# A graph layer on one core: the first gathers' pacing, the node loads' place, and the last tiles' self connection

## The chip, the cores and the metric

The kernel runs on one core of a Trainium2 chip. The metric is device time in microseconds (us), here the median of several executions. Beside it stands one execution taken by the hardware profiler; its span is the time from its first to its last instruction. All arithmetic is float32.

## What is computed

One message-passing layer over a graph of 12500 nodes and 400000 edges, the edges sorted by destination. Each node has 160 features: 64 scalars s and 32 vectors v of three components. Cut to what matters:

```python
h_s, h_v = s @ lin1_ws * a, v @ lin1_wv * a            # per node: the table that is gathered
w = silu(edge_attr_64 @ fc_w1) @ fc_w2                  # per edge: 224 weights
es, ev = h_s[src], h_v[src]                             # per edge: the source's row
mid = products of w, (es, ev) and the edge's 4 attributes
agg = segment_sum(mid, dst)                             # per node
pre = self connection (s @ sc_ws, v @ sc_wv) * a + (agg @ lin2) * a
out = layernorm(x + [silu(pre scalars), sigmoid(pre gates) * pre vectors])
```

The scale factors are left out here. `node_vec1` is the factor a.

## The kernel before

**Setup.** The table h is computed by TensorE and written to memory (L350 to L369). The destinations are made relative to the first one of each block of three tiles (L419, L424). A tile is 128 edges.

**The loop over quads** (L957) takes four tiles a turn: 782 quads, numbered from 0, the last one with a single tile. For each:

- GpSimd gathers the 4 x 128 rows of h with four indirect DMAs (`gather`, L467, the DMA at L471) into one of five buffers `hg`.
- TensorE computes the hidden layer for two quads at a time (`hidden`, L462; ScalarE's SiLU at L464), four quads ahead, and the quad's weights (`weights`, L546) into one of two PSUM banks `pw`.
- VectorE multiplies weights by gathered rows (`products`, L556 and L564), builds a one-hot matrix of the relative destinations (L609) and multiplies it by the edge's attributes (`select_quad`, L618). The attributes arrive in the order of tiles in `eat` (one buffer, 48 tiles) and are copied by ScalarE into the order of quads in `eas` (`by_slot`, L592 and L600). The copy is made when the first quad of such a group of twelve asks for it, in L618.
- Two quads later TensorE sums the products over the edges with the selection as weights (`add_tile`, L625). A finished pair of blocks is copied by ScalarE (L836), turned (L641, L644), put through the second linear map for up to 16 blocks (L654, L657), and added by VectorE into the accumulator `acc` at the block's first node (L662).

**Nodes.** When all edges of 512 nodes are added up, a job finishes them (`finish`, L665). It issues three loads on SP's queue (xs and xv, the transposed features, L682 and L683; xt, the features themselves, L688). Then come two turns, each for two tiles of 128 nodes: TensorE adds the self connection and the accumulator in PSUM (L700 with xs or xv and the weights scs or scv; L701 with acc and the identity), ScalarE takes the tanh (L703), VectorE gates (L708, L711) and adds the features (L717). Then moments (L725, L727), root (L731), norm (L737) and the store (L740). There are 24 jobs, the last of two tiles, and then the last four tiles by themselves behind all edges: these take three of the gather buffers for xt, xs and xv, because the gathers are done.

**Order.** It is written out by hand: each engine runs its instructions in program order. `begin` (L940), called once in each quad behind the products, starts the next job if no turn and no later step of the job before is left and the job's nodes are complete. Its loads are issued at once, and its first turn is run in the next quad by `spread_out` (L912), which puts at most one of four kinds of TensorE work (hidden layer, second map, turning of blocks, turn of nodes) into a half quad. In the last seven quads a turn is run as soon as it is there.

**Pacing.** The third gather of a quad carries an extra dependence: it waits until the last weights of the quad two earlier are done. The dictionary `weighed_by` names that instruction, and it is asked with `.get(n - 2)`, so the first two quads have none.

The indices of the gathers (L160), `eat` (L161) and the edge scalars `es` (L205) are loaded eight quads ahead on SP's queue, the queue of the node loads and stores. An alternative that fetches rows by ScalarE's queue is built for every 900th quad and so for none here.

Of the kernel before, what the change touches and what calls it, by code (L numbers as in the profile page):

```python
# [10 lines left out]
F32 = mybir.dt.float32  # L11
# [50 lines left out]
def gnn_kernel(  # L62
# [104 lines left out]
    def index(t):  # L167
        a0, idx, _ = ahead(t)
        return idx[:, t - a0:t - a0 + 1]
# [492 lines left out]
        nc.vector.tensor_add(window, window, os[:, :, b])  # L662


    def finish(fin, psum, t0, nt, p, most=NF, pool=None):  # L665


        whole = nt if p == P else nt - 1
        if pool is None:
            xt = fin.tile([P, most, D], F32, name="xt")  # L670
            xs = fin.tile([S, most * P], F32, name="xs2")
            xv = fin.tile([V3, most * P], F32, name="xv2")
        else:
            xt, xs, xv = (pool.tile([P, Q, D], F32, name="hg") for _ in range(3))
            xs, xv = (a.rearrange("p t d -> p (t d)")[:k, :most * P] for a, k in ((xs, S), (xv, V3)))
        cn = (nt - 1) * P + p
        held = []
        if whole < nt:
            nc.vector.memset(xt[:, whole], 0.0)
            for a in (xs, xv):  # L680
                nc.vector.memset(a[:, whole * P:nt * P], 0.0)
        nc.sync.dma_start(xs[:, :cn], xs_t[:, t0 * P:t0 * P + cn])  # L682
        nc.sync.dma_start(xv[:, :cn], xv_t[:, t0 * P:t0 * P + cn])  # L683
        parts = [(slice(t0 * P, (t0 + whole) * P), slice(0, whole), P)] if whole else []
        if whole < nt:
            parts.append((slice((t0 + whole) * P, (t0 + whole) * P + p), slice(whole, nt), p))
        for nodes_of, k, n in parts:
            nc.sync.dma_start(xt[:n, k], x[nodes_of, :].rearrange("(t p) d -> p t d", p=n))  # L688

        def turn(ks):  # L690
            if not held:
                held.extend(fin.tile([P, most, *shape], F32, name=name) for name, shape in (
                    ("g", [V3]), ("y", [D]), ("st", [6]), ("mv", [2]), ("rs", [])))
            g, y = held[:2]
            pp = psum.tile([P, 2, 2, V3], F32, name="pp", tag="misc")
            for k in ks:
                c = (t0 + k) * P
                for m, (w, a) in enumerate(((scs, xs), (scv, xv))):
                    at_p = pp[:, k % 2, m]
                    nc.tensor.matmul(at_p, a[:, k * P:(k + 1) * P], w, start=True, stop=False)  # L700
                    nc.tensor.matmul(at_p, acc[:, m, c:c + P], ident[:V3, :V3], start=False, stop=True)  # L701
            for k in ks:
                nc.scalar.activation(g[:, k], pp[:, k % 2, 0], AF.Tanh, scale=half_at[:, t0 + k:t0 + k + 1])  # L703
# [24 lines left out]

        def root():
            mv, rs = held[3:]  # L730
            nc.scalar.activation(rs[:, :nt], mv[:, :nt, 1], AF.Sqrt, bias=eps)  # L731

        def norm():
            _, y, _, mv, rs = held
            nc.vector.reciprocal(rs[:, :nt], rs[:, :nt])
            for k in range(nt):
                nc.vector.tensor_scalar(y[:, k], y[:, k], mv[:, k, 0:1], rs[:, k:k + 1],  # L737
                                        op0=OP.subtract, op1=OP.mult)
            for nodes_of, k, n in parts:
# [9 lines left out]
    jobs = [(t, min(NF, tiles_of_nodes - LAST - t), P)  # L749
            for t in range(0, tiles_of_nodes - LAST, NF)]  # L750
    last_job = (tiles_of_nodes - LAST, LAST, N - (tiles_of_nodes - 1) * P)

    with tc.tile_pool(
        name="fin", bufs=1
# [157 lines left out]
        def spread_out(n, half):  # L912
# [5 lines left out]
            while True:  # L918
                kinds = [(q[0][0] + more, k) for k, (q, more) in enumerate(
                    ((hids_due, 2), (maps_due, 3), (turns_due, 1))) if q and q[0][0] <= n]  # L920
                if not late and turning and half == 0:
                    kinds.append((n + 1, 3))
                if not kinds:
                    return rest
# [12 lines left out]
                else:  # L937
                    return turning.pop(0)()

        def begin():  # L940

            if to_do and not turning and not doing:
                t, nt, p = to_do[0]
                end = (t + nt - 1) * P + p
                if not waiting or min(waiting) * RATE >= end + MARGIN:
                    job = finish(fin, misc_ps, *to_do.pop(0))
                    turning.extend(job[:-3])
                    doing.extend(job[-3:])

        with in_order:  # L950
            fetch(0)
# [5 lines left out]
            for n, (c, i, tiles) in enumerate(steps):  # L957
# [9 lines left out]
                fetch(n + LEAD)  # L967
                fetch_rows(n)
                hg = hq_of.pop(n) if n in own else gather(
                    deep, [index(t) for t, _, _ in tiles], {2: weighed_by.get(n - 2)})  # L970
                pw = weights(pw_ps, hids[c, i // 2], [(half, u - i // 2 * 4) for _, half, u in tiles])
                weighed_by[n] = weighed[-1]

                if n + 4 < len(steps) and not steps[n + 4][1] % 2:
                    hids_due.append((n, n + 4))
                rest = spread_out(n, 0)
                step_on = not rest and doing.pop(0) if doing and not turning and not rest else None
                ready = []
# [18 lines left out]
                    add(*a)  # L997
                if step_on:
                    step_on()
                begin()  # L1000
# [29 lines left out]
            while adds:  # L1030
                for a in add_up(n) + add_up(n):
                    add(*a)
            while turning or doing or to_do:
                begin()
                for f in turning:
                    f()()
                for f in doing:
# [120 lines left out]
```

## Time and profile before

| what | us |
|---|---|
| median of 3 executions | 4024.61 |
| lowest, highest | 4024.17, 4026.55 |
| the profiled execution | 4024.39 |
| its span | 4022.6 |
| GpSimd busy | 2990.6 (74%) |
| TensorE busy | 3566.6 (89%) |
| VectorE busy | 2349.4 (58%) |
| ScalarE busy | 847.9 (21%) |

The profile names engines PE (TensorE), PEld (its weight loads, beside PE), DVE (VectorE), ACT (ScalarE), POOL (GpSimd) and SP or SPq (SyncE's DMA queue). A line of its groups reads: line, engine, operation, out<-in, shapes, count | busy us, mean ns of one | idle us just before them and what ended it. A line in order of time reads: start, duration, engine, line, operation, and in brackets the idle time before it and what ended it. A float32 matmul counts twice, since it runs as two passes. The mean granted TensorE clock was 0.931 of full.

### The profile page before, as it was taken

To read this page: it belongs to the slowest core of one execution; us is meant where nothing else is said; L and a number is where in the kernel's file an instruction comes from. 1 tells how busy PE (TensorE), PEld (TensorE's weight loads), DVE (VectorE), ACT (ScalarE), POOL (GpSimd) and SP (SyncE) were. 2 spreads that over 40 slices of the span, in tenths; PEclk is the share of its full clock that TensorE was granted. 3 is DMA by queue.
4 is the path that set the end of the run, shared out by engine and by line. 5 is a ranking of instruction groups with operands and counts; after the bars stand their busy time and mean duration, and the time that the engine had idled before them with its cause. 6 is when DMAs were issued, how large, how long until landed. Compare 5 with 4: busy or idle time off the path is not lost.

```text
span 4022.6 us, 57806 instructions
## 1 busy us (share of the span) xinstructions
PE 3566.6 (89%) x19989; PEld 1993.0 (50%) x19989; DVE 2349.4 (58%) x6410; ACT 847.9 (21%) x1828; POOL 2990.6 (74%) x3172
## 2 busy tenths in 40 slices
PE   6898898988998988898898898998898888888887
PEld 4454454554554544454454454454454444444445
DVE  5555555555655656556565565665655565656654
ACT  2211212212212212122122121221221221212212
POOL 6777777777777777777777777777777777777773
PEclk8898999989999999899898898998999999999998
DMA  7333434434334434344334334434434344343331
GB/s 236 92 95 98 110 91 102 103 98 109 97 98 103 102 98 103 99 101 104 99 94 110 99 98 103 102 97 104 102 95 107 95 103 105 95 107 101 95 100 53
DMA packets 237525, 412.51 MB, mean 103 GB/s; under 512 B 78040, under 2 KB 160961, under 8 KB 237093
## 3 DMA queue, kind: packets, MB, share of 16 engines
q0 software_dynamic: 152960, 266.64, 25.2%
q1 hardware_dynamic: 83668, 141.96, 14.9%
q8 instruction: 159, 2.61, 0.3%
q14 instruction: 144, 1.18, 0.1%
q10 hardware_dynamic: 594, 0.13, 0.0%
HBM read 392.49 MB, written 16.00 MB: 102 GB/s over the span
## 4 chain that ended last, share of the span: by engine, by line
PE 35%; issue 22%; DMA 17%; POOL 16%; DVE 9%; DVEq 0%; SPq 0%; ACT 0%; POOLq 0%; ACTq 0%
DMA hg<-h_tab,idx 16%; POOL hg L471 16%; PE pa L625 11%; PE pw L546 8%; PE misc L641 6%; DVE pr L564 5%; PE misc L654 4%; PE misc L462 3%; PE misc L701 2%; DVE sel L618 1%; PE misc L700 1%; DVE pr L556 1%; DMA xz<-in_xv_t_dram 1%; DVE acc L662 1%; DVE pw L609 0%
## 5 line engine op out<-in xcount | busy, mean ns | idle before, releaser
L471 POOL DMA_INDIRECT hg<-h_tab,idx x3125 | 2960.0, 947 | 963.8 <-issue 812.1
L625 PE MATMUL pa<-pr,sel 128*64 128x416 f32 x6250 | 1330.0, 548 | 0.5 <-DVE sel L618 0.5
L556 DVE TENSOR_TENSOR pr<-pw,hg 128x512 f32<-128x512 f32 x782 | 540.5, 691 | 1198.8 <-DMA hg<-h_tab,idx 885.0
L564 DVE TENSOR_TENSOR pr<-pw,hg 128x384 f32<-128x384 f32 x2346 | 1154.2, 548 | 0.0
L546 PE MATMUL pw<-w,hid 64*128 64x224 f32 x6250 | 837.6, 388 | 258.2 <-DVE sel L618 254.3
L546 PEld LDWEIGHTS pw<-w,hid 64*128 64x128 f32 x6250 | 553.2, 193 | 809.8 <-DVE sel L618 433.3
L625 PEld LDWEIGHTS pa<-pr,sel 128*64 128x64 f32 x6250 | 393.2, 141 | 685.5 <-issue 661.5
L641 PEld LDWEIGHTS misc<-ident,sa 128*128 128x128 f32 x4168 | 526.5, 205 | 76.8 <-issue 73.4
L641 PE MATMUL misc<-ident,sa 128*128 128x96 f32 (+1 forms) x4168 | 553.3, 289 | 0.7 <-ACT sa L836 0.7
L462 PE MATMUL misc<-es,w 128*128 128x512 f32 (+1 forms) x784 | 442.6, 647 | 19.8 <-DVE rel L424 19.3
L464 ACT ACTIVATE hid<-misc 128x512 f32<-128x512 f32 x392 | 233.7, 596 | 922.8 <-PE misc L462 922.6
L644 ACT COPY tt<-misc 128x512 f32<-128x512 f32 (+1 forms) x263 | 153.1, 582 | 1105.8 <-PE misc L641 1105.8
L654 PE MATMUL misc<-tt,l 128*96 128x256 f32 (+5 forms) x1496 | 358.4, 388 | 0.7 <-ACT tt L644 0.5
L609 DVE TENSOR_TENSOR pw<-rel,iota 128x64 f32<-128x64 int16 x782 | 178.8, 229 | 305.5 <-PE pw L546 275.7
L836 ACT COPY sa<-pa 128x416 f32<-128x416 f32 x521 | 263.0, 505 | 328.1 <-PE pa L625 328.1
L618 DVE TENSOR_TENSOR sel<-pw,eas 128x256 f32<-128x256 f32 x782 | 324.5, 415 | 11.7 <-ACT eas L600 9.7
L654 PEld LDWEIGHTS misc<-tt,l 128*96 128x96 f32 (+1 forms) x1496 | 226.8, 165 | 124.6 <-issue 59.4
L701 PE MATMUL misc<-ident,acc 96*128 96x96 f32 x392 | 109.2, 371 | 142.0 <-DVE acc L662 136.1
L662 DVE TENSOR_TENSOR acc<-acc,os 96x32 f32 x1042 | 196.0, 188 | 22.9 <-ACT os L657 4.5
L462 PEld LDWEIGHTS misc<-es,w 128*128 128x128 f32 x784 | 118.0, 190 | 133.8 <-issue 100.1
L701 PEld LDWEIGHTS misc<-ident,acc 96*128 96x128 f32 x392 | 80.9, 256 | 155.0 <-DVE acc L662 139.8
L657 ACT COPY os<-misc 96x512 f32<-96x512 f32 (+2 forms) x68 | 38.4, 564 | 467.8 <-PE misc L654 363.2
(90 smaller groups left out, 671.0 us busy)
## 6 DMA issues: line engine op xcount, KB each, us to landing
es<-in_es_t_dram SPq DMA_DIRECT2D x258, 384.0 KB
hg<-h_tab,idx POOLq DMA_INDIRECT x3125
h_tab<-ht POOLq DMA_DIRECT2D x24, 320.0 KB
xt<-in_x_dram SPq DMA_DIRECT2D x23, 320.0 KB
out_dram<-y SPq DMA_DIRECT2D x23, 320.0 KB
xv<-in_xv_t_dram SPq DMA_DIRECT2D x23, 192.0 KB
eat<-in_ea_dram SPq DMA_DIRECT2D x41, 96.0 KB
xw<-in_xs_t_dram SPq DMA_DIRECT2D x6, 512.0 KB
```

The source lines that it names most:

```text
L462: nc.tensor.matmul(ph[:k, c], w1[:k, :k], es[:k, t0 * P + c0 * P:t0 * P + c1 * P], start=True, stop=True)
L471: got = nc.gpsimd.indirect_dma_start(out=hg[:, t, :], out_offset=None, in_=h_tab, in_offset=bass.IndirectOffsetOnAxis(ap=i, axis=0))
L546: weighed.append(nc.tensor.matmul(pw[:, t, :NWT], hid[r, c * P:(c + 1) * P], w2[r], start=True, stop=True).ins.name)
L556: nc.vector.tensor_mul(two, pw[:, :n, :2 * S].rearrange("p t (k c) -> p t k c", k=2), hg[:, :n, None, :S].to_broadcast([P, n, 2, S]))
L564: nc.vector.tensor_mul(pr[:, :n, first:first + V3].rearrange("p t (i c) -> p t i c", i=3), pw[:, :n, None, 2 * S + k * V:2 * S + (k + 1) * ...
L618: nc.vector.tensor_mul(sel[:, :n], oh[:, :, None, :].to_broadcast([P, n, 4, W]), by_slot(tiles[0][0])[:, u:u + n, :, None].to_broadcast([P ...
L625: summed.append(nc.tensor.matmul(pa[half * ROWS:(half + 1) * ROWS, :NPR], sel[:, t].rearrange("p k w -> p (k w)"), pr, start=start, stop=s ...
L641: nc.tensor.matmul(pt[:, planes, m * n:(m + 1) * n], sa[:k, c:c + P], wanted[:, of, :n], start=True, stop=True)
L654: nc.tensor.matmul(po[:, k, :nb], l2[r, terms[to, part, four]], a[:, :nb], start=(n == 0), stop=(n == len(of) - 1))
L662: nc.vector.tensor_add(window, window, os[:, :, b])
L701: nc.tensor.matmul(at_p, acc[:, m, c:c + P], ident[:V3, :V3], start=False, stop=True)
L836: nc.scalar.copy(sa, pas.pop(j)[:, :NPR])
```

## The change

Four edits, in the loop and in `finish`:

1. The third gather waits for the weights of two quads earlier only from quad 6 on (`n >= 6`), where it did from quad 2 on.
2. `begin` loads a job one ahead: as soon as no turn is left it calls `finish` for the next job, which issues its loads, and keeps it; the job starts when its nodes are complete and the job before is through, and its first turn comes two quads later (in the last seven quads, at once). Nothing of this before quad 18.
3. The self connection of the last four tiles is computed at quads 13 (loads) and 17 (two matmuls of 468 columns with scs and scv as stationary operand, two additions into `acc`). Their turns at the end then have L701 alone. Only xt still goes into a gather buffer there, and the fills of xs and xv are gone.
4. The copy of the edge attributes is asked for three quads ahead, before the other work of the quad.

The core of the diff:

```diff
+    def connect_last(psum, c0, cn, xs, xv):
+        for k, (w, a) in enumerate(((scs, xs), (scv, xv))):
+            p = psum.tile([V3, 512], F32, name="psc", tag="misc")
+            nc.tensor.matmul(p[:, :cn], w, a[:, :cn], start=True, stop=True)
+            nc.vector.tensor_add(acc[:, k, c0:c0 + cn], acc[:, k, c0:c0 + cn], p[:, :cn])
...
+        connect = pool is None and t0 + nt < tiles_of_nodes
...
+                for m in range(2):
+                    if connect:
+                        w, a = ((scs, xs), (scv, xv))[m]
+                        nc.tensor.matmul(pp[:, k % 2, m], a[:, k * P:(k + 1) * P], w,
+                                         start=True, stop=False)
+                    nc.tensor.matmul(pp[:, k % 2, m], acc[:, m, c:c + P], ident[:V3, :V3],
+                                     start=not connect, stop=True)
...
-                if not late and turning and half == 0:
+                if not late and turning and half == 0 and n >= turn_from[0]:
...
-        def begin():
-            if to_do and not turning and not doing:
-                t, nt, p = to_do[0]
+        loaded_job, turn_from = [], [0]
+        def begin(n):
+            if turning or n < 18:
+                return
+            if to_do and not loaded_job:
+                loaded_job.append((to_do[0], finish(fin, misc_ps, *to_do.pop(0))))
+            if loaded_job and not doing:
+                (t, nt, p), job = loaded_job[0]
                 end = (t + nt - 1) * P + p
                 if not waiting or min(waiting) * RATE >= end + MARGIN:
-                    job = finish(fin, misc_ps, *to_do.pop(0))
+                    loaded_job.clear()
                     turning.extend(job[:-3])
                     doing.extend(job[-3:])
+                    turn_from[0] = n + 2
...
+                if n == 13:
+                    last_own = own_scalars_vectors(fin, *last_nodes)
+                if n == 17:
+                    connect_last(misc_ps, *last_nodes, *last_own)
...
                 hg = hq_of.pop(n) if n in own else gather(
-                    deep, [index(t) for t, _, _ in tiles], {2: weighed_by.get(n - 2)})
+                    deep, [index(t) for t, _, _ in tiles], {2: weighed_by[n - 2] if n >= 6 else None})
...
+                if n + 3 < len(steps):
+                    by_slot(steps[n + 3][2][0][0])
```

`own_scalars_vectors` issues the loads of xs and xv. In the changed kernel the lines after L665 move: L700 and L701 become L709 and L711, L703 becomes L714, L740 becomes L751, L836 becomes L848, and the two new matmuls are L677.

More of the change, by code (lines that the diff above doesn't have):

```diff
@@ L662, in add, with own_scalars_vectors @@
         nc.vector.tensor_add(window, window, os[:, :, b])
+    def own_scalars_vectors(pool, c0, cn):
+        xs = pool.tile([S, NF * P], F32, name="xs2")
+        xv = pool.tile([V3, NF * P], F32, name="xv2")
+        nc.sync.dma_start(xs[:, :cn], xs_t[:, c0:c0 + cn])
+        nc.sync.dma_start(xv[:, :cn], xv_t[:, c0:c0 + cn])
+        return xs, xv
+    def connect_last(psum, c0, cn, xs, xv):
[3 more added lines that the diff above has]
+            nc.vector.tensor_add(acc[:, k, c0:c0 + cn], acc[:, k, c0:c0 + cn], p[:, :cn])
     def finish(fin, psum, t0, nt, p, most=NF, pool=None):
+        connect = pool is None and t0 + nt < tiles_of_nodes
         whole = nt if p == P else nt - 1
[L669 to L676, printed above, removed]
+        xt = fin.tile([P, most, D], F32, name="xt") if pool is None else pool.tile([P, Q, D], F32, name="hg")
+        if connect:
+            xs, xv = own_scalars_vectors(fin, t0 * P, nt * P)
         held = []
@@ L679, in finish @@
             nc.vector.memset(xt[:, whole], 0.0)
[L680 to L683, printed above, removed]
         parts = [(slice(t0 * P, (t0 + whole) * P), slice(0, whole), P)] if whole else []
@@ L697, in turn @@
                 c = (t0 + k) * P
[L698 to L701, printed above, removed]
+                for m in range(2):
+                    if connect:
+                        w, a = ((scs, xs), (scv, xv))[m]
[3 more added lines that the diff above has]
+                                     start=not connect, stop=True)
             for k in ks:
@@ L751, in gnn_kernel @@
     last_job = (tiles_of_nodes - LAST, LAST, N - (tiles_of_nodes - 1) * P)
+    last_nodes = last_job[0] * P, N - last_job[0] * P
     with tc.tile_pool(
@@ L999, in gnn_kernel @@
                     step_on()
-                begin()
+                begin(n)
                 some_rows(SLOTS[1])
@@ L1032, in gnn_kernel @@
                     add(*a)
-            while turning or doing or to_do:
-                begin()
+            while turning or doing or to_do or loaded_job:
+                begin(n)
                 for f in turning:
```

## The prediction

> **What bounds the kernel now.** I read the page first (busy time, then the groups), then what GpSimd waited for, then its queue in order of time at the start and the end of the span, and last the other engines in those two places. The page:
>
> ```profile
> span 4022.6 us, 57806 instructions
> PE 3566.6 (89%) x19989; PEld 1993.0 (50%) x19989; DVE 2349.4 (58%) x6410; ACT 847.9 (21%) x1828; POOL 2990.6 (74%) x3172
> L471 POOL DMA_INDIRECT hg<-h_tab,idx x3125 | 2960.0, 947 | 963.8 <-issue 812.1 <-DMA hg<-h_tab,idx 55.8 <-PE pw L546 21.8
> L556 DVE TENSOR_TENSOR pr<-pw,hg 128x512 f32<-128x512 f32 x782 | 540.5, 691 | 1198.8 <-DMA hg<-h_tab,idx 885.0 <-issue 290.9 <-DVE pw L609 12.7
> ```
>
> TensorE is the busiest by share, which tempts one to call it the bound. The third and fourth lines say otherwise: VectorE stood idle 885.0 us for gathered rows, and the 3125 gathers fill 2960.0 us with 963.8 us of idle before them, of which 812.1 us is called issue. Is that idle time a wait or a price of each gather? What GpSimd waited for, and its queue in order of time, decide it:
>
> ```profile
> POOL hg L471 <- issue: 812.1, 2666, 0.3
> POOL hg L471 <- PE pw L546: 21.8, 43, 8.9
> 52.15 1.05 POOL L471 DMA_INDIRECT hg<-h_tab,idx  x1 [3.42 <-DMA scv<-in_sc_wv_dram]
> 63.53 0.94 POOL L471 DMA_INDIRECT hg<-h_tab,idx  x1 [0.30 <-issue]
> 73.33 0.94 POOL L471 DMA_INDIRECT hg<-h_tab,idx  x1 [8.85 <-PE pw L546]
> 74.58 0.94 POOL L471 DMA_INDIRECT hg<-h_tab,idx  x1 [0.31 <-issue]
> 3971.52 0.95 POOL L471 DMA_INDIRECT hg<-h_tab,idx  x1 [0.30 <-issue]
> ```
>
> Each gather costs 0.947 + 0.30 = 1.25 us, and behind the first gather only one gap is longer than about half a microsecond, that of 8.85. From 73.33 to 3971.52 run 3114 intervals: 3898.19 / 3114 = 1.252 us, so GpSimd never stops for anybody in that stretch. **The kernel is bound by the issue of gathers.** The work of the other engines is hidden under it, except in two places: ahead of 73.33 (where GpSimd has one wait of 8.85 us), and after the last gather, 51 us before the end of the span.
>
> **Third gather.** Quads of four tiles are numbered from 0. From quad 2 on, the third gather waits until the weights (L546) of two quads earlier are done. The gather at 73.33 is the eleventh (52.15 plus nine intervals of some 1.25 us gives the tenth, at 63.53): the third of quad 2, waiting for the weights of quad 0. After the change quads 2 to 5 have no such wait. The gap falls from 8.85 to the usual 0.30 us: **-8.55 us**, if GpSimd meets no later wait. Three others could take its place, each to be read at times moved 8.55 us forward:
>
> ```profile
> 71.19 1.86 PE L546 MATMUL pw<-w,hid 64*128 64x224 f32 x8
> 82.53 1.03 PE L546 MATMUL pw<-w,hid 64*128 64x224 f32 x8 [0.56 <-DVE sel L618]
> 86.09 1.03 PE L546 MATMUL pw<-w,hid 64*128 64x224 f32 x8
> 73.97 1.48 DVE L564 TENSOR_TENSOR pr<-pw,hg 128x384 f32<-128x384 f32 x3
> 92.20 0.69 DVE L556 TENSOR_TENSOR pr<-pw,hg 128x512 f32<-128x512 f32 x1 [1.84 <-DMA hg<-h_tab,idx]
> ```
>
> - Weights: quad 6 is the first that waits. Its third gather is number 26 (from 0), due at 64.78 + 16 x 1.25 = 84.8. The weights of quad 4 (second line) end at 83.56: 1.2 us ahead. Quad 7 is due at 89.8, the weights of quad 5 end at 87.12. From one to the next TensorE needs 3.56 us and GpSimd 5.0, so the margin grows.
> - Buffers: there are five, so the first gather of quad 5, due at 77.28, needs the products of quad 0, which end at 75.45. Margin 1.8 us, and it grows alike.
> - Queue: as built, a gather waits for the one eight before it to land; that is 10 us. A slow landing in the chain of waits, beside a load of edge scalars, took 7.10:
>
> ```profile
> 3854.98 7.10 DMA hg<-h_tab,idx
> ```
>
> From 92.20 on rows are what is late, so what comes sooner is used, and the 8.55 us is carried to the tail unchanged. Ends: 0 and 8.55; I take 8.55.
>
> **Loads one job ahead, tail.** In order of time, after the last gather:
>
> ```profile
> 3976.56 1.03 PE L546 MATMUL pw<-w,hid 64*128 64x224 f32 x8
> 3979.57 0.47 SPq L682 DMA_DIRECT2D xs<-in_xs_t_dram  x1
> 3982.00 0.74 PE L700 MATMUL misc<-scs,xs 64*128 64x96 f32 x2 [4.41 <-DMA xs<-in_xs_t_dram]
> 3986.53 1.28 ACT L703 ACT_TABLE_LOAD   x1 [9.28 <-PE misc L701]
> 3988.29 0.57 ACT L600 COPY eas<-eat 128x4 f32<-128x4 f32 x5
> 3988.89 0.42 DVE L618 TENSOR_TENSOR sel<-pw,eas 128x256 f32<-128x256 f32 x1 [9.70 <-ACT eas L600]
> ```
>
> The job of two tiles is loaded only when the norm of the job before is out, and TensorE stands still 4.41 us for it. With the loads issued after that earlier job's last turn (around 3956 here), the data lie ready 20 us ahead: **-4.41 us**. All other jobs lose nothing now: this is the only wait of its kind in the list of waits, so 23 of 24 loads bring nothing. What is late next? The windows around it, and the turn (L700, L701) of an earlier job for comparison:
>
> ```profile
> 3953.65:3955.90 2.25, 2.25 (x18) 1.88 (x19) 0.93 (x2) 0.00 (x0) 1.71 (x2) 1.00 0.26 71
> 3977.60:3982.00 4.40, 0.00 (x1) 0.00 (x1) 1.55 (x7) 0.00 (x0) 0.00 (x0) 0.95 0.42 117
> 3982.00:3988.40 6.40, 6.40 (x22) 4.47 (x24) 0.00 (x0) 1.86 (x5) 0.00 (x0) 0.50 0.09 23
> 3988.40:3996.20 7.80, 7.66 (x54) 5.00 (x50) 6.33 (x28) 2.03 (x10) 0.00 (x0) 1.00 0.00 0
> 3996.20:4001.90 5.70, 3.83 (x32) 3.35 (x32) 1.08 (x6) 2.02 (x4) 0.00 (x0) 1.00 0.37 105
> 4001.93:4010.04 8.11, 8.07 (x30) 6.80 (x30) 2.01 (x8) 2.51 (x5) 0.00 (x0) 0.51 0.08 23
> ```
>
> Columns: stretch, its length, busy us of PE, PEld, DVE, ACT, POOL, then the granted clock. Behind the idle stretch TensorE runs 6.40 us at 0.50; the turn takes 4.45 us where the same work at 1.00 took 2.25, and the L625 behind it 2.54 where it takes 1.55:
>
> ```profile
> 3955.90 1.55 PE pa L625 x8
> 3986.45 2.54 PE pa L625 x8
> ```
>
> If the clock stays at 1.00 without the idle stretch, that is 2.20 + 0.99 = **-3.19 us** more. Ends: 0 and 3.19. I take 3.19, because the half clock starts at the end of the idle stretch (0.95 within it). Behind the turn TensorE has work of its own up to 3996.20 (7.66 of 7.80 us busy in the fourth line), so it, and not the gate on ScalarE and VectorE, ends this stretch: 6.40 + 7.80 - 3.19 = 11.0 us from 3977.6, that is 3988.6 instead of 3996.2.
>
> The Trainium skill's page "TensorE: Matmul & The Clock Gate", Part 1, says that the clock drops to half after about 3.4 us without work and is given back after about as long of work. The trace agrees on the drop (4.40 us idle, then 0.50) and shows 6.40 us until the return. By that rule the full clock is kept here, and the sum is the same; for the last stretch it gives another result, which is a rival below.
>
> **Edge attributes.** The 9.70 us wait of VectorE above looks like the copies' price and is not: they take 0.57 us, queued on ScalarE behind the turn, thus behind xs. Copied three quads earlier the selection and first product pass in front of the gate, but TensorE is what ends this stretch, so I add **0** (ends 0 and 1.0: the copies and part of the selection). The earlier copy needs eat landed. In the middle of the span:
>
> ```profile
> 2056.89 0.33 SPq L160 DMA_DIRECT2D idx<-in_src_dram  x1
> 2057.33 0.36 SPq L161 DMA_DIRECT2D eat<-in_ea_dram  x1
> 2109.96 0.81 ACT L592 COPY eas<-eat 128x32 f32<-128x32 f32 x6
> ```
>
> eat is issued at 2057.33 and copied at 2109.96; three quads (15 us) sooner still leaves 37 us. The copies (0.81 us a group) lie in ScalarE's 79% of idle time; without that cover they would still not be on GpSimd's path.
>
> **Self connection.** The last tiles' eight products with scs and scv leave the last chain; the chain of waits from 4001.9 to 4010.1 gives them 45.3% of 8.2 us:
>
> ```profile
> by line: PE misc L701 53.3%; PE misc L700 45.3%; ACT g L703 4.2%; issue 0.8%
> ```
>
> That is **-3.71 us** at half clock. At full clock the remaining L701 (53.3%, 4.37 us) would halve, 2.2 us more; I don't take it, since the clock there was 0.51. What is added: at quad 17 two products of 468 columns and two additions. The nearest rows:
>
> ```profile
> L462 PE MATMUL misc<-es,w 128*128 128x512 f32 (+1 forms) x784 | 442.6, 647 | 19.8 <-DVE rel L424 19.3 <-ACT hid L464 0.5
> ```
>
> 784 passes for 392 calls: 442.6 / 392 = 1.1 us a call, so about 2.2 us on TensorE and, at the L556 mean of 0.69 us, 1.4 us on VectorE, once, under the gathers. Uncovered they would cost 3.6 us. Two loads move from the end to SP's queue at quad 13, ahead of a chunk's edge scalars; they wait for nothing there. Two fills go, beside other work before.
>
> **Sum.** The profiled execution took 4024.39 us: span 4022.6 and 1.79 around it; it stands 0.22 under the median 4024.61. 8.55 + 4.41 + 3.19 + 0 + 3.71 = 19.86. 4024.39 - 19.86 = **4004.5 us**.
>
> **Rivals.**
> - *The front wait comes back.* The 1.2 us margin at quad 6 is thin: if the extra gathers delay the edge scalars of the next chunk and with them TensorE, GpSimd loses each us beyond the margin for good, up to 8.55: 4013.0. Against it, the issue of those scalars and their use (the L462 of quad 6) lie 12.7 us apart:
>
> ```profile
> 64.12 11.28 SPq L205 DMA_DIRECT2D es<-in_es_t_dram  x4
> 76.79 1.13 PE L462 MATMUL misc<-es,w 128*128 128x512 f32 x2
> ```
>
> - *Full clock in the last stretch.* TensorE was busy 3.83 of 5.70 us ahead of it, never idle as long as 4.4 us, and yet got 0.51. If that hung on chance, the L701 halve: 4004.5 - 2.2 = 4002.3. Against it: the change takes work out of just that stretch (the first L700), so it is emptier still. By the rule of the Trainium skill's page "TensorE: Matmul & The Clock Gate", Part 1, this rival is right, since 3.4 us without work don't occur there; the profiled execution has spoken against the rule once.
> - *The tail finds another wait.* If something other than xs holds the last turn, only the front is left: 4024.39 - 8.55 = 4015.8. For it: much is queued there; against it, the chain above is busy from 3982 on.
> - *Nothing arrives.* If VectorE and TensorE needed the slack that GpSimd's pause gave, both go: 4024.4. Against it: 885 us of waits for rows.
> - *Slower.* A node load now waits on SP's queue for the gate and turn of the job before, with the indices of later gathers behind it. Indices issued at 2056.89 belong to the quad that VectorE selects at 2109.96; GpSimd is at most five buffers (25 us) ahead of that, so 28 us are spare. If the load holds SP longer, GpSimd stops, and 24 jobs at more than 27.9 / 24 = 1.2 us beyond the spare time make it slower than 4032.7. A gate is done within a quad or two (10 us), so this is unlikely.
>
> **How the numbers follow.** Forecast 0.62 (own range 4003 to 4008: below by the 1.0 of the copies and selection and 0.4 of spread between the runs, above by the 3.19 lost); full clock at the end 0.14; front wait back 0.11, some of it under 4012; tail wait 0.07; nothing 0.03; slower 0.03. The range 4001 to 4012 takes the forecast, either clock in the last stretch (4002.3 less the same 1.4 is 4000.9) and, with the clock as forecast, most of a lost front. A change under 0.2% (8 us) is about what a measurement can't tell from none: faster 0.94, same 0.03, slower 0.03.
>
> **What would show it.** Right: gathers 1.25 us apart from 52 on with no gap of 8 us, last gather near 3963; L709 without a wait for xs and at clock 1.00; the selection without 9.70; eight L711 in some 4.4 us at the end. Wrong: a gap on GpSimd at quads 5 to 12, a new wait in front of L709, L654 or the last additions, or idx late in the middle.

## The result, and the profile after

| | before | after |
|---|---|---|
| median of 6 executions, us | 4024.73 | 4003.86 |
| lowest, highest | 4022.81, 4026.55 | 4001.70, 4007.72 |
| the profiled execution | 4024.39 | 4003.13 |
| its span | 4022.6 | 4001.4 |
| mean granted clock | 0.931 | 0.932 |

The ratio of the medians is 0.995, with a 95% interval of 0.9937 to 0.9963: the changed kernel is 20.9 us faster, 4003.86 us where 4004.5 was forecast. First the page of the changed kernel:

```profile
span 4001.4 us, 57827 instructions
PE 3566.7 (89%) x19977; PEld 1990.9 (50%) x19977; DVE 2349.7 (59%) x6410; ACT 853.0 (21%) x1828; POOL 2988.6 (75%) x3172
L471 POOL DMA_INDIRECT hg<-h_tab,idx x3125 | 2958.1, 947 | 956.2 <-issue 805.4
```

The busy times are those of before, nearly to a microsecond: nothing was made cheaper, instructions were moved. GpSimd's idle time before gathers fell from 963.8 to 956.2 us. Next its longest wait for weights, in the view of waits, where the last column is the longest single one:

```profile
POOL hg L471 <- PE pw L546: 14.5, 47, 0.4
```

The longest was 8.9 us before and is 0.4 now. In order of time, the first gather, the eleventh and the last:

```profile
52.04 1.05 POOL L471 DMA_INDIRECT hg<-h_tab,idx  x1 [4.50 <-DMA h_tab<-ht]
...
64.66 0.94 POOL L471 DMA_INDIRECT hg<-h_tab,idx  x1 [0.30 <-issue]
...
3960.87 0.95 POOL L471 DMA_INDIRECT hg<-h_tab,idx  x1 [0.30 <-issue]
```

The eleventh gather follows the tenth at the usual 0.30 us, and the last starts 10.65 us earlier than before (3971.52). Behind it TensorE, in order of time:

```profile
3965.92 1.03 PE L546 MATMUL pw<-w,hid 64*128 64x224 f32 x8
3966.78 0.35 PE L709 MATMUL misc<-scs,xs 64*128 64x96 f32 x2
...
3969.13 1.62 PE L625 MATMUL pa<-pr,sel 128*64 128x416 f32 x8
...
3972.26 2.44 PE L654 MATMUL misc<-tt,l 128*96 128x96 f32 x22
...
3975.47 2.31 PE L625 MATMUL pa<-pr,sel 128*64 128x416 f32 x10
3978.43 1.08 PE L641 MATMUL misc<-ident,sa 128*128 128x96 f32 x8 [0.65 <-ACT sa L848]
3979.97 3.36 PE L654 MATMUL misc<-tt,l 128*96 128x64 f32 x22 [0.46 <-ACT tt L644]
3984.61 3.73 PE L711 MATMUL misc<-ident,acc 96*128 96x96 f32 x16 [1.28 <-DVE acc L662]
```

The second line has no bracket: the turn of the two-tile job follows the weights at once, where before TensorE stood still 4.41 us for xs. The L625 behind it takes 1.62 us. The last line is the turns of the last four tiles: 3.73 us, where L700 and L701 together ran from 4001.93 to 4010.00. But the line above it, the last maps, takes 3.36 us. In the same view of the kernel before, that L625 and those last maps were:

```profile
3986.38 2.61 PE L625 MATMUL pa<-pr,sel 128*64 128x416 f32 x8
...
3998.29 2.36 PE L654 MATMUL misc<-tt,l 128*96 128x64 f32 x22 [0.46 <-ACT tt L644]
```

The windows of the changed kernel show the clock there (the number behind the five engines is the granted clock):

```profile
3966.78:3969.13 2.35, 2.35 (x18) 1.97 (x16) 2.28 (x10) 0.00 (x0) 0.00 (x0) 1.00 0.01 3
3978.43:3980.00 1.57, 1.11 (x9) 1.00 (x9) 0.00 (x0) 0.37 (x1) 0.00 (x0) 1.00 0.00 0
3980.00:3981.40 1.40, 1.40 (x12) 1.28 (x12) 0.00 (x0) 0.00 (x0) 0.00 (x0) 0.83 0.00 0
3981.40:3983.30 1.90, 1.90 (x11) 1.68 (x10) 0.00 (x0) 0.00 (x0) 0.00 (x0) 0.50 0.00 0
3984.60:3988.30 3.70, 3.69 (x16) 3.49 (x16) 0.86 (x4) 2.52 (x5) 0.00 (x0) 0.50 0.15 47
```

The turn runs at 1.00 now (first line). The clock falls at about 3981.4, in the middle of the last maps, while TensorE is at work; before, it fell behind them. One wait is new, on VectorE:

```profile
3988.24 0.29 DVE L719 SCALAR_TENSOR_TENSOR y<-g,misc 128x128 f32<-128x128 f32 x1 [2.08 <-DMA out_dram<-y]
```

The gate of the last four tiles waits for the store of the two-tile job to leave the one buffer y.

To compare kernels, the rest of this document uses a **tail**: from the start of the last L546 with eight rows (3965.92 above) to the end of the last norm (L748; L737 before). It was 38.25 us before (3976.56 to 4014.81) and is 27.59 now (3965.92 to 3993.51). The two profiled executions differ by 21.26 us: 10.65 in the start of the last gather, 10.66 in the tail, -0.05 in the rest.

### The profile page after: what moved, and what is told of

Read it like the earlier page. It is cut to its first block, busy times and chain, and to the rows that moved or that the text cites. A ratio compares the mean times of both kernels' runs of the same rounds, so it can differ in the third digit from the quotient of the medians.

```text
span 4001.4 us, 57827 instructions
## 1 busy us (share of the span) xinstructions
PE 3566.7 (89%) x19977; PEld 1990.9 (50%) x19977; DVE 2349.7 (59%) x6410; ACT 853.0 (21%) x1828; POOL 2988.6 (75%) x3172
## 4 chain that ended last, share of the span: by engine, by line
PE 41%; issue 20%; DMA 15%; POOL 14%; DVE 9%; DVEq 0%; ACT 0%; POOLq 0%; ACTq 0%
DMA hg<-h_tab,idx 15%; POOL hg L471 14%; PE pa L625 14%; PE pw L546 9%; PE misc L641 6%; DVE pr L564 5%; PE misc L654 4%; PE misc L462 4%; PE misc L711 2%; PE misc L709 1%; DVE sel L618 1%; DVE pr L556 1%; DVE acc L662 0%; POOL h_tab L366 0%; DVE pw L609 0%
## 5 line engine op out<-in xcount | busy, mean ns | idle before, releaser
L471 POOL DMA_INDIRECT hg<-h_tab,idx x3125 | 2958.1, 947 | 956.2 <-issue 805.4
L625 PE MATMUL pa<-pr,sel 128*64 128x416 f32 x6250 | 1335.1, 550 | 0.5 <-DVE sel L618 0.5
L546 PE MATMUL pw<-w,hid 64*128 64x224 f32 x6250 | 839.7, 389 | 258.4 <-DVE sel L618 256.8
L546 PEld LDWEIGHTS pw<-w,hid 64*128 64x128 f32 x6250 | 554.8, 194 | 812.3 <-DVE sel L618 413.2
L625 PEld LDWEIGHTS pa<-pr,sel 128*64 128x64 f32 x6250 | 393.9, 141 | 687.8 <-issue 663.8
L654 PE MATMUL misc<-tt,l 128*96 128x256 f32 (+5 forms) x1496 | 355.7, 386 | 2.0 <-DVE y L722 1.5
L848 ACT COPY sa<-pa 128x416 f32<-128x416 f32 x521 | 262.8, 504 | 351.3 <-PE pa L625 350.2
L654 PEld LDWEIGHTS misc<-tt,l 128*96 128x96 f32 (+1 forms) x1496 | 226.1, 165 | 124.0 <-issue 58.7
L711 PE MATMUL misc<-ident,acc 96*128 96x96 f32 x392 | 106.4, 368 | 123.1 <-DVE acc L662 123.1
L711 PEld LDWEIGHTS misc<-ident,acc 96*128 96x128 f32 x392 | 79.4, 254 | 135.5 <-DVE acc L662 126.9
```

What stands on the lines that cost most here:

```text
L471: got = nc.gpsimd.indirect_dma_start(out=hg[:, t, :], out_offset=None, in_=h_tab, in_offset=bass.IndirectOffsetOnAxis(ap=i, axis=0))
L546: weighed.append(nc.tensor.matmul(pw[:, t, :NWT], hid[r, c * P:(c + 1) * P], w2[r], start=True, stop=True).ins.name)
L625: summed.append(nc.tensor.matmul(pa[half * ROWS:(half + 1) * ROWS, :NPR], sel[:, t].rearrange("p k w -> p (k w)"), pr, start=start, stop=s ...
L654: nc.tensor.matmul(po[:, k, :nb], l2[r, terms[to, part, four]], a[:, :nb], start=(n == 0), stop=(n == len(of) - 1))
L711: nc.tensor.matmul(pp[:, k % 2, m], acc[:, m, c:c + P], ident[:V3, :V3], start=not connect, stop=True)
L848: nc.scalar.copy(sa, pas.pop(j)[:, :NPR])
```

## The experiments

**The chips.** The first four kernels below ran on a chip on which the kernel before took 4024.78 us (33 executions), as in the result above. The other eight ran on two others: e2, e6, e7 and e9 on one where it took 4692.96 us, e6b, e7b, e9b and e10 on one where it took 4692.54 us (27 executions on each). These two are alike and are called the slower chips here. There TensorE, far more than GpSimd, sets the time. The chain of work that ended last, by engine, and two groups of e10 (the last experiment, and one of the quickest kernels there) show it:

```profile
PE 64%; issue 11%; DVE 11%; another core or an unknown queue 10%; POOL 3%; DMA 2%; ACT 0%; DVEq 0%; SPq 0%; POOLq 0%; ACTq 0%
...
L471 POOL DMA_INDIRECT hg<-h_tab,idx x3125 | 2955.0, 946 | 1640.1 <-issue 817.8 <-remote 458.7 <-PE pw L546 152.1
L625 PE MATMUL pa<-pr,sel 128*64 128x416 f32 x6250 | 1577.6, 579 | 146.0 <-issue 142.3
```

In the changed kernel on the first chip the same chain is PE 41%, DMA 15%, POOL 14%. A gather costs as much as there, but GpSimd idles 1640.1 us ("remote" is a release that the profile can't place, "another core or an unknown queue" in the chain); TensorE's L625 takes 579 ns in place of 550 and loses 142.3 us to pauses that the profile calls issue (no such wait shows on the first chip, where L625 idles 0.5 us). So the expected times of those eight, made for the first chip, are not tested by their medians. What can be compared is their tails, each in one execution: in ten kernels, on all three chips, the tail starts 5.03 to 5.06 us after the last gather (17.1 in the one without pacing), and its rows at full clock have the durations seen above. Neither the kernel before nor the changed one has a profile from the slower chips, so the tails there are held against those of the first chip.

**e1: edit 1 alone.**

```diff
-                    deep, [index(t) for t, _, _ in tiles], {2: weighed_by.get(n - 2)})
+                    deep, [index(t) for t, _, _ in tiles], {2: weighed_by[n - 2] if n >= 6 else None})
```

> The kernel before with edit 1 alone: the third gather waits for weights from quad 6 on. Theory (gathers are the bound, GpSimd's pause of 8.85 us shrinks to 0.30 and nothing gives it back): 4024.7 - 8.55 = 4016.2 us, no gap of over 1 us between gathers behind the first. Rival (the pause was slack that the other engines take back): 4024.7.

Measured: 4016.87 us, ratio 0.9981 (0.9972 to 0.999), 7.9 us less. The waits of GpSimd for weights:

```profile
POOL hg L471 <- PE pw L546: 10.8, 35, 0.4
```

The long one is gone, the last gather starts at 3961.51, and the wait for xs (4.55 us) is still there. The front's gain reaches the end of the kernel. The tail, in which nothing was edited, is 39.88 us, 1.63 longer than before's, mostly because the clock fell already within the last maps:

```profile
3988.64 3.54 PE L654 MATMUL misc<-tt,l 128*96 128x64 f32 x22 [0.46 <-ACT tt L644]
```

So the tail alone differs by more than 1.5 us between executions, and a difference between two tails says something only where the rows show where it comes from.

**e3: edit 2 alone.**

```diff
-        def begin():
-            if to_do and not turning and not doing:
+        loaded_job, turn_from = [], [0]
+        def begin(n):
+            if turning or n < 18:
+                return
+            if to_do and not loaded_job:
+                loaded_job.append((to_do[0], finish(fin, misc_ps, *to_do.pop(0))))
```

> The kernel before with edit 2 alone: node loads one job ahead. Theory (wait of 4.41 us for xs goes and TensorE's clock stays at 1.00 behind it; but with the attribute copies still queued behind the turn, the gate reads PSUM about 1.2 us later than TensorE could use it): about 4024.7 - 6.4 = 4018.3, granted clock 1.00 through the turn. Rival (only the wait goes, the clock falls anyway): 4020.3, clock 0.5 in the turn.

Measured: 4017.19 us, ratio 0.9983 (0.9974 to 0.9992), 7.6 us less. The profiled execution was a long one (4027.29); its gathers took 950 ns each in place of 947. Its tail is 31.74 us, 6.51 less than before. TensorE, in order of time:

```profile
3993.44 2.41 PE L654 MATMUL misc<-tt,l 128*96 128x96 f32 x22 [1.03 <-DVE y L711]
```

The wait for xs is gone and the clock is 1.00 up to 4000. What is late next is VectorE, whose selection waits for the copies of the edge attributes, with the gate behind it: 1.03 us on TensorE, as this expectation had it (1.2). That wait, and not a fault of the loads, makes up nearly all of the 1.1 us by which this tail falls short of the 7.6 of the prediction.

**e4: edit 3 alone.**

```diff
+                if n == 13:
+                    last_own = own_scalars_vectors(fin, *last_nodes)
+                if n == 17:
+                    connect_last(misc_ps, *last_nodes, *last_own)
```

> The kernel before with edit 3 alone: self connection of the last four tiles added at quads 13 to 17. Theory: the products with scs and scv leave the last chain, 3.7 us at half clock: 4021.0; the two matmuls and two additions at quad 17 cost nothing, since gathers are the bound. Rival (the additions at quad 17 and the store or the gate hold the end): 4024.7 or more.

Measured: 4024.06 us, ratio 0.9999 (0.999 to 1.0008), from 4020.77 to 4042.2: less than expected, and by its interval not told from 4021. The profiled execution was the longest, 4042.2 us: gathers of 950 ns again, and a tail of 41.72 us, 3.5 longer than before. Its last turns and its windows, clock behind the engines as above:

```profile
4021.79 3.73 PE L711 MATMUL misc<-ident,acc 96*128 96x96 f32 x16 [1.29 <-DVE acc L662]
```

```profile
3994.60:3999.00 4.40, 4.40 (x18) 3.72 (x18) 0.00 (x0) 0.00 (x0) 0.00 (x0) 0.50 0.30 85
4002.00:4007.00 5.00, 5.00 (x24) 4.22 (x22) 4.73 (x19) 0.88 (x2) 0.00 (x0) 0.50 0.00 0
4010.70:4014.80 4.10, 4.10 (x11) 1.23 (x10) 0.19 (x1) 0.37 (x1) 0.00 (x0) 0.55 0.00 0
4017.00:4020.50 3.50, 3.47 (x22) 3.06 (x22) 0.00 (x0) 0.00 (x0) 0.00 (x0) 0.62 0.00 0
```

The eight removed products are gone (3.73 us, as in the changed kernel). But behind the wait for xs the clock stayed at half for 20 us, in which TensorE did not pause, where before it came back after 6.4. In this execution that cost more than the edit saves. Whether it is so in most executions of e4, one profile can't tell.

**e5: edit 4 alone.**

```diff
+                if n + 3 < len(steps):
+                    by_slot(steps[n + 3][2][0][0])
                 rest = spread_out(n, 0)
```

> The kernel before with edit 4 alone: edge attributes copied three quads ahead. Theory (VectorE's 9.70 us wait for the copies is at root a wait for xs, and TensorE ends that stretch at half clock): 4024.7, at most 1 us less; the wait of 9.70 becomes one of the gate. Rival (the wait is worth its face value): 4015.0.

Measured: 4024.11 us, ratio 0.9998 (0.9989 to 1.0007); tail 38.15 us (38.25 before). The wait has moved to the gate (8.22 us for the tanh), as expected. The rival (9.7 us for the selection's wait) is out.

**e6 and e6b: all but the copies** (the changed kernel without the two lines of e5; run twice, once on each of the slower chips).

> The changed kernel with the attribute copies made late again. Theory: with xs there and the clock at 1.00, the last copies stand between the tanh and the selection and delay the gate, so L654 begins about 1.3 us later: 4005.2. Rival (face value of the wait before): 4013.6. Second rival (no effect at all): 4003.9.

> The changed kernel without the early copies of the edge attributes, on a chip on which the kernel before takes about 4025 us. Theory: the copies alone were worth 0.6 us or nothing (4024.11 against 4024.78), because in the kernel before the loads of xs were late anyway; with the loads early the copy before the selection of the two-tile job's step would come back as a wait of 1.0 to 1.3 us: 4005.2, and the ScalarE wait before that selection shows again. Rival: the copies carry more than that once the rest is there, because the four parts measured alone add up to 16.9 us of the 20.9 us: 4008 or more. Second rival: nothing, 4003.9.

Measured: 4685.51 us, ratio 0.9989 (0.998 to 0.9998), and 4689.47, ratio 0.9992 (0.9982 to 1.0002). VectorE and TensorE of e6, in order of time, a fence for each:

```profile
4651.69 0.42 DVE L618 TENSOR_TENSOR sel<-pw,eas 128x256 f32<-128x256 f32 x1 [3.08 <-ACT eas L600]
```

```profile
4653.42 2.41 PE L654 MATMUL misc<-tt,l 128*96 128x96 f32 x22 [1.03 <-DVE y L722]
```

And TensorE of e6b:

```profile
4656.92 3.23 PE L654 MATMUL misc<-tt,l 128*96 128x96 f32 x22 [1.03 <-DVE y L722]
...
4661.69 3.94 PE L625 MATMUL pa<-pr,sel 128*64 128x416 f32 x10
```

Both have the wait that the copies hide: 3.08 us on VectorE, 1.03 of it left on TensorE. In e6 the clock held behind it (2.41); in e6b it fell (3.23, then 3.94 for the L625 that takes 2.31 at full clock). The tails are 28.18 and 32.17 us, against 27.59 in the changed kernel. So without the copies the tail is 0.6 us longer in one execution and 4.6 in the other. Of that the 1.03 us of the wait is the copies' share that the rows show. Whether the half clock behind it in e6b is theirs too is open: e3, e6 and both runs of e7 below have the same wait, and the clock held behind it in all four. While xs is late, the copies are worth nothing that shows (e5).

**e2: all but the pacing** (the changed kernel with `weighed_by.get(n - 2)` again).

> The changed kernel with the old pacing (third gather waits from quad 2 on). Theory: the front's 8.55 us come back, 4003.9 + 8.55 = 4012.4, with the gap of about 8.9 us before the eleventh gather. Rival (the tail's gains need the earlier start): between 4013 and 4024.7.

Measured, on a slower chip: 4685.26 us, ratio 0.9988 (0.9978 to 0.9998). With GpSimd idle 1640 us there, a gap at the front says nothing; the expected 4012.4 was not put to the test. Its tail, with the same work as the changed kernel's, is 27.07 us: the clock fell behind the last maps (2.36 us) in place of within them (3.36). So there the tail has its gains without the earlier start.

**e7 and e7b: the kernel before, TensorE kept busy while it waits for xs** (the same kernel twice, once on each of the slower chips).

```diff
+            if t0 == 92:
+                for _ in range(5):
+                    nc.tensor.matmul(pp.rearrange("p a m c -> p (a m c)"), ident,
+                                     l2[:, :4].rearrange("p m c -> p (m c)"), start=True, stop=True)
```

> The kernel before with five idle products (identity times the second linear map's weights, overwritten by the next matmul) put in front of the job of two tiles: TensorE computes something that is thrown away for about 4.2 us while it waits for xs. Theory (the clock falls because TensorE stands idle there): granted clock 1.00 through the turn, turn in 2.25 us, and 4024.7 - 2.2 = 4022.5, since the copies and the gate then hold L654. Rival (the clock falls there for another reason): clock 0.5, 4024.7 or some tenths more.

> The kernel before, with five thrown-away matmuls of 128 x 384 on TensorE while it waits for the xs of the two-tile job; nothing of the change. Theory: the clock falls because TensorE stands still; kept busy, the clock stays at 1.00 through the two-tile job and the sums behind it, the job takes 2.25 us in place of 4.45 and the first sums 1.62 in place of 2.5, so 4021.6 to 4022.5 against 4024.7. Rival: the clock falls at that place whatever TensorE does, for another reason: 4024.7 and a clock of 0.50 there.

Measured: 4693.82 us, ratio 1.0004 (0.9995 to 1.0013), and 4694.92, ratio 1.0005 (0.9996 to 1.0014); no difference shows there, with intervals of some 4 us either way where 2.2 us were expected. The tails are 36.43 and 36.45 us, 1.8 less than before's 38.25 on the first chip. TensorE of e7, in order of time, and the windows of its turn:

```profile
4640.71 3.49 PE L698 MATMUL misc<-l,ident 128*128 128x384 f32 x10
4645.21 0.46 PE L704 MATMUL misc<-scs,xs 64*128 64x96 f32 x2 [1.00 <-DMA xs<-in_xs_t_dram]
...
4647.66 1.62 PE L625 MATMUL pa<-pr,sel 128*64 128x416 f32 x8
...
4651.89 2.41 PE L654 MATMUL misc<-tt,l 128*96 128x96 f32 x22 [1.03 <-DVE y L715]
```

```profile
4645.21:4647.66 2.45, 2.45 (x16) 2.08 (x16) 0.00 (x0) 0.00 (x0) 0.00 (x0) 1.00 0.23 62
```

xs lands as late as ever, but the clock stays at 1.00: the turn takes 2.45 us in place of 4.45, the L625 behind it 1.62 in place of 2.6. The four profiled executions in which TensorE stood idle there (before, e1, e4, e5) all have the half clock behind it, the two in which it was kept busy do not: the half clock of that place comes with TensorE's idleness. Of the 3.19 us 1.8 reach the end, since TensorE then meets the wait that the copies hide (1.03).

**e9 and e9b: the changed kernel with no pacing at all** (the same kernel twice, once on each of the slower chips).

```diff
-                    deep, [index(t) for t, _, _ in tiles], {2: weighed_by[n - 2] if n >= 6 else None})
+                    deep, [index(t) for t, _, _ in tiles])
```

> The changed kernel with no pacing of the gathers at all. Theory: behind quad 6 the wait holds GpSimd once, for 0.14 us at the end, so nothing changes: 4003.9 (within 1 us). Rival (the pacing keeps gathers from crowding other loads in the steady state): slower, with longer waits of TensorE for edge scalars or of GpSimd for landings.

> The changed kernel with no gather waiting for weights at all, on a chip on which the gathers set the time. Theory: the gathers run one behind another at 1.251 us in any case, so that nothing changes: 4003.9, within 2 us, and GpSimd's wait for buffers stays under 30 us in all. Rival, from the run on the chip on which TensorE set the time and this kernel took 5169 us in place of 4686: without the waits the gathers crowd something else, and the kernel is up to 10% slower here too: 4100 to 4410.

Measured: 5169.22 us, ratio 1.1007 (1.0989 to 1.1025), and 5183.0, ratio 1.1043 (1.1021 to 1.1065). What GpSimd waits for, and TensorE's largest group, in e9b:

```profile
POOL hg L471 <- DVE pr L564: 1199.4, 250, 6.5
```

```profile
L625 PE MATMUL pa<-pr,sel 128*64 128x416 f32 x6250 | 1699.0, 610 | 261.3 <-issue 256.1 <-ACT sa L848 2.3 <-DVE sel L618 0.5
```

Unpaced, GpSimd runs ahead until all buffers are full and waits for products; the last gather is 17.1 us ahead of the last weights, not 5.03. With it TensorE is slower: L625 takes 610 ns (e10: 579), with pauses of 256.1 us (142.3), at a mean clock of 0.837 (0.892). So on these chips, where TensorE sets the time, the waits for weights are worth some 10%. By which path the unpaced gathers slow TensorE, and whether anything of it holds on the first chip, stays open; neither theory was tested where it was meant to be.

**e10: the changed kernel, TensorE kept busy to the end, and a buffer of its own for the last y.**

```diff
+        own_y = pool.tile([P, Q, D], F32, name="hg") if pool else None
...
+            def keep_busy(k):
+                pw = pw_ps.tile([P, Q, 256], F32, name="pw").rearrange("p q c -> p (q c)")
+                for _ in range(k):
+                    nc.tensor.matmul(pw[:, :V3 * 2], ident, l2[:, :2].rearrange("p m c -> p (m c)"),
+                                     start=True, stop=True)
```

> The changed kernel, with seven thrown-away matmuls of 128 x 192 in the gaps of TensorE before its last three groups (two before the last turning, one before the last maps, four before the last job), and with the last job's y in a buffer of its own, so that its gate need not wait for the store of the two-tile job. Theory: the clock fell at 3981.5 in the changed kernel because TensorE had worked too little in the microseconds before, not because of one gap of 0.65 us; with the gaps filled the clock stays 1.00 to the end: the last maps take 2.36 in place of 3.36 us, the last job about 2.4 in place of 3.73, the gate does not wait, and the kernel takes 4001.0 to 4002.4 in place of 4003.9. Rival: the clock falls there whatever TensorE does: 0.50 at the end again, and only the 0.4 us of the store are gained: 4003.5.

Measured, on a slower chip: 4685.36 us, ratio 0.9989 (0.998 to 0.9998). Its TensorE at the end, and two windows:

```profile
4660.44 0.57 PE L1052 MATMUL pw<-l,ident 128*128 128x192 f32 x2
4661.07 2.36 PE L654 MATMUL misc<-tt,l 128*96 128x64 f32 x22
4663.27 1.52 PE L1052 MATMUL pw<-l,ident 128*128 128x192 f32 x8
4664.71 2.02 PE L713 MATMUL misc<-ident,acc 96*128 96x96 f32 x16
```

```profile
4661.00:4663.40 2.40, 2.35 (x24) 2.20 (x24) 0.00 (x0) 0.02 (x1) 0.00 (x0) 1.00 0.02 7
4663.30:4666.73 3.43, 3.43 (x26) 3.05 (x24) 1.55 (x7) 3.16 (x5) 0.00 (x0) 1.00 0.01 2
```

The clock is 1.00 to the last matmul: maps 2.36 us (3.36), turns 2.02 (3.73), and the gate waits no more for the store. The tail is 25.56 us, 2.03 less than the changed kernel's (1.51 less than e2's) and the shortest of all. By that, 4001.8 us would follow on the first chip; there it was not run, and on the slower chips its ratio can't be told from e2's 0.9988. So a version that beats the changed kernel is made likely by its tail, not shown by its time.

The clock in the tails, by the duration of the same four groups (us):

| kernel | first L654 | L625, ten rows | second L654 | last L711 (e10: L713) | tail |
|---|---|---|---|---|---|
| before | 2.41 | 2.31 | 2.36 | with L700 | 38.25 |
| e1 | 2.44 | 2.31 | 3.54 | with L700 | 39.88 |
| after | 2.44 | 2.31 | 3.36 | 3.73 | 27.59 |
| e9 | 2.44 | 2.31 | 3.61 | 3.73 | 27.84 |
| e9b | 2.44 | 2.31 | 3.38 | 3.73 | 28.43 |
| e2 | 2.44 | 2.31 | 2.36 | 3.73 | 27.07 |
| e6 | 2.41 | 2.31 | 2.88 | 3.73 | 28.18 |
| e6b | 3.23 | 3.94 | 3.65 | 3.73 | 32.17 |
| e10 | 2.44 | 2.31 | 2.36 | 2.02 | 25.56 |

## Why the prediction was right, point by point

**The bound.** Right on the first chip: the gathers issue at 1.25 us from the first to the last (3124 intervals in 3908.83 us), and what was gained at the front arrived at the end. On the two chips with a slower TensorE it does not hold, which the trace of before could not tell.

**Front, -8.55.** Right: 8.85 became 0.30, no other gap took its place, and the margins of 1.2 and 1.8 us held (longest wait for weights 0.4). The rival of a returning wait falls with it. The last gather came 10.65 us earlier; beside the 8.55, 0.11 is an earlier first gather, and the remaining 2.0 is nearly all the gathers' own time (2958.1 against 2960.0 us), which e5, without this edit, has as well (2958.5). It is spread between executions, and no gain of the change.

**Loads ahead, -4.41 and -3.19.** The size is right, the account is not quite. The L625 with ten rows ends at 3977.78 where it ended at 3996.10: 18.32 earlier, 10.65 of it from the gathers, so 7.67 against the 7.60 of the sum. But e3 shows the loads alone giving 6.51 in the tail. The sentence that TensorE has work of its own behind the turn overlooked that the second part of this work, L654, waits for the gate (L711), which without edit 4 stands behind the copies; a wait of 1.03 us appears there, in e3, e6, e6b, e7 and e7b alike. That the clock's part is real, and comes with the idle stretch, e7 shows with xs as late as ever.

**Copies, 0.** Right that the 9.70 us were not their price (e5: nothing). Wrong in the sum: once the loads are early, they carry 1.03 of the 7.60 that was booked under the loads. The upper end, 1.0, was that size. It left out the clock: in e6b the same 1.03 us was followed by the half clock and the tail was 4 us longer than in e6, in one of the five executions with this wait.

**Self connection, -3.71.** The mechanism held, the net was 2.98. The turns themselves gave more: 8.07 us to 3.73, -4.34. Two things took some back: the clock fell within the last maps (+1.00), and the gate waited for the store (+0.36 from the last L711 to the end of the norm, 4.81 before and 5.17 after). The single y buffer is in the code and was not priced. The first of the two is not the edit's doing by what the runs show: in e1, which lacks it, the clock fell within the last maps as well (3.54 us). In e4 alone the gain was not measurable.

**Full clock in the last stretch** (the rival with 0.14): it did not occur, as forecast. Where e10 brings it about, the turns take 2.02 us in place of 3.73, 1.7 less where the rival had 2.2. The longest idle time of TensorE in the 15 us before the fall at 3981.4 was 0.65 us. The Trainium skill's page "TensorE: Matmul & The Clock Gate", Part 1, gives as its working rule that idle gaps of over about 3.4 us cost the clock; by that rule the clock would have held, and the trace disagrees. The same section says that activity is judged in a free-running window of that length, and tells of the warm-up that it is therefore run-variable. A moment that varies fits the table above, since nearly the same work meets the fall within the last maps (after, e1, e6, e9, e9b), behind them (before, e2) or already within the maps before (e6b). That the window is what decides is argued here, not shown; shown is that TensorE kept the clock where its gaps were filled (e7, e7b behind the wait for xs, e10 to the end).

**Slower** (0.03): it did not occur, but the reason given against it was wrong. The prediction had a node load wait some 10 us on SP's queue, with 28 us to spare; in the changed kernel SP's 23 waits of this kind add to 828.8 us, the longest 37.8. Still no gather waits over 0.4 us. In the kernel before, the loads of the edge scalars held the same queue as long (33.6 us at most, 2967.9 in all, now 2323.9), and the indices of the middle are issued at 2046.38 where they were at 2056.89, earlier by as much as the gathers are.

**The sum.** 19.86 forecast, 21.26 between the two profiled executions: 2.1 more in the gathers, 0.65 less in the tail (10.66 where 11.31 was summed), the rest around the span. The medians differ by 20.87, and the interval of their ratio leaves 14.9 to 25.4 us. That the forecast came within 1 us is thus in part luck: some 2 us of the gathers' spread, which is no gain of the change, stand against 1.0 us that the earlier fall of the clock took, and another execution may have neither. The parts alone add to 7.9 + 7.6 + 0.7 + 0.7 = 16.9 us, with intervals of some 4 us either way on each, so that their sum is not told from 20.9. That the copies are worth something only once the loads are early would be 1 us of the difference.

## What to carry to other kernels

Find the one engine that never stops, and price a change only by what reaches its first or last instruction: here all but some 2 of the 21.3 us between the two profiled executions came from one wait ahead of the steady state and from the 51 us behind it, with the busy times nearly unchanged. In a tail, price a wait together with the clock that it may cost, and ask of each wait that goes what is 1 us behind it: the copies were worth nothing that showed until the loads were early. Edits that unblock each other should be tried together and by leaving one out, not only one at a time.

## What the runs showed of the hardware

- In the changed kernel the clock fell to half with no idle time of TensorE over 0.65 us in the 15 us before, and in one execution (e4) stayed at half through 20 us of work; filling gaps of 0.5 to 1.3 us with thrown-away matmuls kept it at 1.00 in the one execution of e10 that was profiled.
- The same gathers cost 947 ns in most executions on the first chip and 950 in others (e3, e4): 3 ns in 3125 gathers are 9 us, as much as the largest of the four edits brought, and most of the 10.1 us by which e3's profiled execution lies above its median.
- The same program took 4024.78 us on one chip, 4692.96 and 4692.54 on two others, with the gathers alike (947 ns before, 946 in e10) and TensorE slower, by its granted clock (0.929 against 0.888 and 0.889, medians of before's executions) and by pauses between its own instructions (e10: 142.3 us before L625 alone). What makes the difference, the runs don't tell. There e2, e6, e6b and e10, the kernels nearest to the changed one, were 0.08 to 0.12% faster than before by their medians (e6b's interval includes no difference); the changed kernel itself was not run there.
- Taking away the waits that hold the gathers back made the kernel 10% slower on those two chips (e9, e9b).
